# A list scheduler's price for a change of ScalarE's table, raised in two places

## The chip, the cores and the metric

One core of a Trainium2 chip runs the whole program. The metric is the device time of one execution in microseconds (us), as the median of several runs. The core has five engines that run their own instruction streams side by side: TensorE (PE in the profile, with its weight loads as PEld), VectorE (DVE), ScalarE (ACT), GpSimd (POOL) and SyncE (SP, which here issues DMAs).

## The reference

Four attention modules follow each other on x, which holds 32 sequences of 64 tokens with 256 features, all in float32. A second input, ctx, has the same shape. In short:

```
x = L0(x, ctx)        # norm, 8 heads of 64, softmax, output product, residual
x = L1(x, ctx)        # 16 heads of 16; keys and values from layer_norm(ctx); gated residual
x = L2(ctx, x)        # queries from x, keys and values from concat(ctx, x); then
                      #   rmsnorm and gelu(out @ w1 + b1) @ w2 + b2, residual
x = L3(x, ctx)        # layer norm and masked self-attention; layer norm and
                      #   cross-attention; layer norm and gelu perceptron, residuals
softmax: exp(scores - max) / sum
gelu:    the tanh form; w1 is 256 x 1024, w2 is 1024 x 256
```

So Exp is wanted by every softmax, and GELU by the two perceptrons, those of L2 and of L3. L2's rmsnorm takes a Square.

## The kernel before

**Stages.** L0 is written in an order laid out by hand, with the set-up of later weights mixed in. Everything after it, the modules L1, L2 and L3 (L3's self-attention and its cross-attention count apart, so that there are four layers l = 0 to 3 of the loop), is first recorded and then ordered by a planner, the class `Plan`. In the trace that part begins at about 455 us.

**Groups and sets.** The 2048 tokens are cut into 8 groups of 256. Attention is done in 80 "sets" of 128 tokens: 16 for L1, 32 for L2, 16 for L3's self-attention, 16 for its cross-attention. A set runs through scores on TensorE (`a_scores`, four PSUM banks "s"), for L3 a mask (`a_mask`, VectorE and GpSimd), the maximum (`a_max`), the subtraction (`a_sub`), one Exp of 128x1024 on ScalarE (`a_exp`), the sum (`a_sum`), scaling (`a_scale`, GpSimd, or `a_rows`), transposes (`a_turn`), the product with the values (`a_values`) and the way out (`a_fin`). Three tiles "E" serve the sets in turn.

**Perceptrons.** `mlp_steps` makes four steps for each group of L2 and of L3, so 64 in all. A step's `up` makes a product into a PSUM bank of the "pj" ring, of which there are four, applies GELU to it in two ACTIVATEs of 128x256 (tile "u"), casts it on ScalarE (xThh) and takes the rest on VectorE (xTlh). Its `down` makes the second product, which adds up over the four steps. L2's rmsnorm ahead of its perceptron (`post_b`) has two Squares in a group (tile "rb" from "boot").

**The planner.** `link` turns the recorded operations into atoms with their dependencies, `cost` gives each atom a duration, and, on ScalarE, a form: "gelu" for GELU, "exp" for Exp and Square, none for copies and for the plain ACTIVATEs. `order` then builds the program: it keeps a clock of its own for each engine (`free`), and for every engine it looks at the atoms whose dependencies are placed. A candidate's start is the latest of the engine's clock, its inputs and the freeing of its tiles. On ScalarE a candidate whose form differs from the one last placed gets an addition to its start. The earliest start wins on each engine; among equal starts the due date decides (`urgent`, with a random part of up to 0.5 from a fixed seed, 4), and over the engines the earliest again. When the atom is placed and the form changes, a second addition goes to its start, which moves ScalarE's clock and all that depends on the atom. So both additions count in the planner's clock, and the first counts in the comparison too. The planner's times never reach the chip: they only fix each engine's order of instructions, which the chip then follows with its own durations. The loads of the tables themselves aren't written by the kernel; they are put in where the order needs them.

The same order binds TensorE, VectorE, ScalarE, GpSimd and the DMA issues of SyncE. Weights of later layers are loaded and prepared in the course of it (`load_unit`: DMA, scaling on GpSimd, a cast on ScalarE, the rest on GpSimd or VectorE), at sets fixed by `load_at`.

Of the kernel before, what the change touches and what calls it, by code (L numbers as in the profile page):

```python
# [93 lines left out]
class Plan:  # L94
# [194 lines left out]
    def order(self, atoms):  # L289
        ties = random.Random(self.SEED)  # L290
        first, left, queue, turn = {}, {}, {}, {}
        for at in atoms:
            at.takes, at.written = [], False
            for r in at.roots:
                r.__dict__.setdefault("users", []).append(at)
                if r not in first and r.at is None:
                    first[r] = at
                left[r] = left.get(r, 0) + 1

        for r, at in first.items():  # L300
            src = [b for b in at.before if b.root is not None and b.root.psum and b.key == "T" and not r.psum] if at.key != "T" else []
            owner = src[-1] if src else at
            r.owner = owner
            owner.takes.append(r)
        for at in atoms:
            for r in at.takes:
                queue.setdefault(r.slot, []).append(r)
        for at in atoms:
            at.takes += [r for r in at.roots if r.at is None and r not in at.takes]
        live = {slot: list(rs) for slot, rs in self.early.items()}  # L310
        gone = {r: 0.0 for rs in live.values() for r in rs if r not in left}
        free = {k: 0.0 for k in self.engines}
        form = {}
        ready = {k: [] for k in self.engines}
        for at in atoms:
            at.wait = len(at.before)
            at.at = 0.0
            at.urgent = at.due + ties.uniform(0, self.TIE) - (3.0 if at.key in "VA" and any(isinstance(x, View) and x.root.psum for o in at.ops for x in o.ins) else 0.0)
            if not at.wait:
                ready[at.key].append(at)  # L320
        out = []

        def slots(at):

            t = 0.0
            need = {}
            at.takes = [r for r in at.takes if r.at is None]
            if at.key == "T" and any(r.tag == "pj" for r in at.takes) and len(at.root.users) > 1:
                us = at.root.users
                if not us[1].key == "T" and any(not x.written and x not in us for b in us for x in b.before):  # L330
                    return None
            for r in at.takes:
                need.setdefault(r.slot, []).append(r)
            for s, rs in need.items():
                q = queue[s]
                if any(r not in q[:self.RING.get(s[1], 1) + len(rs) - 1] for r in rs):
                    return None
                have = live.setdefault(s, [])
                over = len(have) + len(rs) - rs[0].bufs
                if over > 0:  # L340
                    ends = sorted(gone[r] for r in have if r in gone)
                    if len(ends) < over:
                        return None
                    t = max(t, ends[over - 1])
            return t
        n = len(atoms)
        while len(out) < n:
            best = None
            for e, rs in ready.items():
                cand = []  # L350
                for at in rs:
                    s = slots(at)
                    if s is None:
                        continue
                    t = max(free[e], at.at, s)
                    if at.form is not None and e == "A" and form.get(e) not in (None, at.form):
                        t += 0.4
                    cand.append((t, at))
                if not cand:
                    continue  # L360
                t0 = min(t for t, _ in cand)
                t, at = min(((t, at) for t, at in cand if t <= t0), key=lambda x: (x[1].urgent, x[1].index))
                if best is None or t < best[0]:
                    best = (t, at)
            if best is None:
                stuck = [(k, at.due, at.ops[0].method, [r.slot for r in at.takes]) for k, rs in ready.items() for at in rs]
                raise RuntimeError(f"no order: {len(out)} of {n}, {stuck[:20]}")
            t, at = best
            e = at.key
            ready[e].remove(at)  # L370
            d = at.time
            if at.form is not None:
                if form.get(e) not in (None, at.form):
                    d += 0.12 if e == "T" else 0.0
                    if e == "A":
                        t += 0.9
                form[e] = at.form
            for r in at.takes:
                have = live[r.slot]
                if len(have) >= r.bufs:  # L380
                    old = min((x for x in have if x in gone), key=lambda x: gone[x])
                    have.remove(old)
                    r.at = old.at
                else:
                    r.at = min(set(range(r.bufs)) - {x.at for x in have})
                have.append(r)
                queue[r.slot].remove(r)
            at.start = t
            free[e] = t + d
            end = t + d + at.late  # L390
            at.end = end
            for r in at.roots:
                left[r] -= 1
                r.last = max(getattr(r, "last", 0.0), end)
                if not left[r]:
                    gone[r] = r.last
            for b in at.after:
                b.wait -= 1
                b.at = max(b.at, (t + d if b.key == e else end) + 0.06 * (b.key != e))
                if not b.wait:  # L400
                    ready[b.key].append(b)
            at.written = True
            out.append(at)
        self.atoms = out
        return out
# [1269 lines left out]
```

## Time and profile before

| what | value |
|---|---|
| median of 3 runs | 1130.74 us (1130.67 to 1131.31) |
| the profiled execution | 1132.07 us |
| its span | 1130.3 us, 35569 instructions |
| mean granted clock of TensorE | 0.987 |
| busy: PE, DVE, ACT, POOL | 1067.8, 894.9, 906.3, 761.8 us |
| loads of ScalarE's table in the planned part | 45, together 57.7 us |
| DMA | 41.21 MB, mean 36 GB/s |

The page gives each engine's busy time, the span in 40 slices (28.3 us each), the chain of work that ended last and the costliest groups. In a group's line the name of the operation is followed by what it writes and reads, the count, the busy time in us, the mean in ns, and the idle time of the engine just before these instructions. L156 marks the instructions of L0 and L125 those that went through the planner's recorder. A busy TensorE isn't a TensorE at its peak, since the ends of its matmuls are modelled.

### The profile page before, as it was taken

Reading aid. Unit: us, or ns where it says so; the run is one execution under the profiler, and the core shown is the slowest. Engines: PE = TensorE matmul, PEld = TensorE weight load, DVE = VectorE, ACT = ScalarE, POOL = GpSimd, SP = SyncE. Lnnn points to the kernel's source line nnn. Section 1 sums busy time; section 2 is a strip of 40 time slices with the busy share of each in tenths; the row PEclk is TensorE's granted clock in tenths of the full one; section 3 lists DMA queues with packets and bytes.
Section 4 is the critical chain, followed back from the end, with each engine's and each line's share of the span. In section 5 each row is a group of like instructions: output and inputs, shape, how many; then the busy total and the mean of one; then the engine's idle time right before and its main releaser. Section 6 shows DMA issues by size and latency. Waiting matters only on the chain.

```text
span 1130.3 us, 35569 instructions
## 1 busy us (share of the span) xinstructions
PE 1067.8 (94%) x14396; PEld 872.2 (77%) x14396; DVE 894.9 (79%) x1575; ACT 906.3 (80%) x2326; POOL 761.8 (67%) x829
## 2 busy tenths in 40 slices
PE   6999999999999999899999999999999988889998
PEld 4666666666666666788898989998988877779998
DVE  4889989897888777688888878777878878777842
ACT  2888888887888789577778889889898777888974
POOL 3788888886778667635546634477866989996520
PEclk9999999999999999899999999999999989989999
DMA  3001211111110100311211100000000111110000
GB/s 96 21 25 36 61 35 49 35 34 44 34 34 25 34 16 2 93 37 58 68 47 47 34 26 26 21 29 22 21 20 21 49 51 51 43 34 21 11 20 29
DMA packets 41300, 41.21 MB, mean 36 GB/s; under 512 B 7059, under 2 KB 37796, under 8 KB 41136
## 3 DMA queue, kind: packets, MB, share of 16 engines
q1 hardware_dynamic: 40816, 38.54, 10.9%
q8 instruction: 114, 1.87, 0.7%
q10 hardware_dynamic: 320, 0.40, 0.1%
q14 instruction: 50, 0.41, 0.1%
HBM read 26.30 MB, written 2.10 MB: 25 GB/s over the span
## 4 chain that ended last, share of the span: by engine, by line
PE 59%; DVE 15%; ACT 10%; POOL 10%; issue 4%; DMA 0%; SPq 0%; DVEq 0%; POOLq 0%; ACTq 0%
PE pj L125 39%; PE pt L156 6%; ACT E L156 5%; PE av L156 5%; PE sc L156 4%; PE s L125 4%; DVE mx L156 3%; POOL E L125 3%; DVE E L125 2%; DVE PT L156 2%; ACT PT L156 2%; DVE sB L156 2%; POOL E L156 2%; DVE mx L125 2%; PE pt L125 1%
## 5 line engine op out<-in xcount | busy, mean ns | idle before, releaser
L156 POOL TENSOR_TENSOR E<-E,rs 128x512 f32<-128x512 f32 x256 | 263.5, 1040 | 84.0 <-DVE rs L156 64.5
L156 ACT ACTIVATE E<-sc,mx 128x256 f32<-128x256 f32 x512 | 238.4, 481 | 23.2 <-DVE rs L156 21.9
L156 DVE TENSOR_REDUCE mx<-sc 128x4 f32<-128x1024 f32 x128 | 155.8, 1217 | 2.8 <-PE sc L156 1.4
L156 PE MATMUL sc<-cd,T 64*128 64x256 f32 x1024 | 144.0, 400 | 10.5 <-ACT E L156 10.0
L125 POOL TENSOR_TENSOR E<-E,sm 128x512 f32<-128x512 f32 x96 | 101.1, 1078 | 68.9 <-DVE sm L125 56.1
L156 PE MATMUL av<-PT,us 128*64 128x256 f32 x1024 | 125.0, 385 | 0.0
L156 PEld LDWEIGHTS pt<-ident,E 64*128 64x128 f32 x2048 | 83.6, 139 | 43.6 <-POOL E L156 15.8
L156 PEld LDWEIGHTS av<-PT,us 128*64 128x64 f32 x1024 | 68.3, 136 | 54.7 <-issue 20.4
L156 PEld LDWEIGHTS sc<-cd,T 64*128 64x128 f32 x1024 | 89.6, 189 | 25.8 <-ACT E L156 17.8
L125 DVE TENSOR_REDUCE sm<-E 128x16 f32<-128x1024 f32 (+1 forms) x80 | 96.0, 1200 | 15.3 <-ACT E L125 15.3
L156 ACT ACTIVATION_READ_ACCUMULATOR E<-sc,mx 128x1 f32 x512 | 108.0, 211 | 0.0
L156 PE MATMUL pt<-ident,E 64*128 64x64 f32 x2048 | 98.2, 228 | 6.1 <-ACT PT L156 2.2
L125 ACT COPY PTe<-pj 128x512 f32<-128x512 f32 x160 | 88.0, 590 | 19.2 <-PE pj L125 17.1
L125 PE MATMUL pj<-ident,E 128*128 128x128 f32 x640 | 90.8, 281 | 8.0 <-DVE rb L125 2.5
L156 ACT COPY PT<-pt 128x512 f32<-128x512 f32 x128 | 75.6, 591 | 24.3 <-PE pt L156 22.8
L125 PE MATMUL pj<-w,xThh 128*128 128x256 f32 x512 | 93.4, 287 | 0.1
L125 PE MATMUL pj<-xThn,w 128*128 128x256 f32 x512 | 92.2, 285 | 0.7 <-DVE rb L125 0.4
L156 DVE COPY PT<-pt 128x512 f32<-128x512 f32 x128 | 86.0, 672 | 5.2 <-PE pt L156 5.1
L125 ACT ACTIVATE E<-E 128x1024 f32<-128x1024 f32 x80 | 84.9, 1062 | 5.8 <-DVE E L125 4.6
L125 PEld LDWEIGHTS pj<-ident,E 128*128 128x128 f32 x640 | 71.6, 143 | 16.7 <-issue 3.6
L125 DVE TENSOR_TENSOR xTlh<-u,xThh 128x512 fp32r<-128x512 f32 x64 | 54.8, 861 | 29.9 <-ACT xThh L125 29.5
L156 DVE RECIPROCAL rs<-sm 128x2 f32<-128x2 f32 x256 | 40.1, 156 | 46.5 <-ACT E L156 43.7
(223 smaller groups left out, 2798.3 us busy)
## 6 DMA issues: line engine op xcount, KB each, us to landing
kb<-kfm SPq DMA_DIRECT2D x44, 128.0 KB
xd<-in_x SPq DMA_DIRECT2D x32, 128.0 KB
cd<-in_ctx SPq DMA_DIRECT2D x32, 128.0 KB
boot<-in_ctxT SPq DMA_DIRECT2D x16, 256.0 KB
kb<-kfm SPq DMA_DIRECT2D x64, 64.0 KB
xt<-in_x SPq DMA_DIRECT2D x16, 128.0 KB
boot<-in_ctx SPq DMA_DIRECT2D x8, 256.0 KB
out<-x SPq DMA_DIRECT2D x8, 256.0 KB
```

Of the source, the lines that this page charges most:

```text
L125: getattr(self.engines[o.key], o.method)(*[real(x) for x in o.p], **{k: real(x) for k, x in o.k.items()})
L156: return f(*p, **k)
```

## The change

Two numbers in `order`. The addition in the comparison goes from 0.4 to 0.9 us, the addition when the atom is placed from 0.9 to 1.28 us. In all a change of the table moves the planner's clock by 2.18 us where it moved it by 1.3. Nothing else in the source differs; the order of all instructions after L0 is worked out anew from these numbers, with the same seed.

```diff
                     t = max(free[e], at.at, s)
                     if at.form is not None and e == "A" and form.get(e) not in (None, at.form):
-                        t += 0.4
+                        t += 0.9
                     cand.append((t, at))
...
                 if form.get(e) not in (None, at.form):
                     d += 0.12 if e == "T" else 0.0
                     if e == "A":
-                        t += 0.9
+                        t += 1.28
                 form[e] = at.form
```

## The prediction

> **What bounds the kernel now.** I read the page first: busy times and the 40 slices.
>
> ```profile
> PE 1067.8 (94%) x14396; PEld 872.2 (77%) x14396; DVE 894.9 (79%) x1575; ACT 906.3 (80%) x2326; POOL 761.8 (67%) x829
> ...
> PE   6999999999999999899999999999999988889998
> ...
> POOL 3788888886778667635546634477866989996520
> PEclk9999999999999999899999999999999989989999
> ```
>
> TensorE (PE) is busy in all but the last tenth of nearly every slice; the exceptions lie around slice 16 (where layer 0 ends, 455 us) and in slices 32 to 35, where POOL rises to 9 and the granted clock falls. Only what stands after 455 us is ordered by the planner, so I cut that part by what ScalarE (ACT) does in it, in the view of busy time by stretch:
>
> ```profile
> 455.00:600.00 145.00, 137.18 (x2544) 121.97 (x2546) 119.42 (x172) 102.63 (x210) 78.11 (x89) 0.98 0.19 59
> 600.00:875.00 275.00, 268.99 (x4293) 245.38 (x4281) 219.90 (x319) 242.85 (x471) 166.18 (x167) 1.00 0.08 26
> 875.00:1010.00 135.00, 118.97 (x1723) 104.90 (x1722) 105.46 (x169) 105.34 (x220) 126.48 (x128) 0.92 0.14 45
> 1010.00:1061.00 51.00, 50.04 (x656) 47.33 (x655) 43.25 (x55) 46.08 (x85) 36.62 (x31) 1.00 0.06 19
> 1061.00:1130.30 69.30, 65.28 (x630) 64.14 (x630) 29.91 (x52) 42.60 (x88) 13.43 (x20) 0.99 0.07 24
> ```
>
> After the stretch and its length the columns are busy PE, weight loads, DVE, ACT, POOL, the clock, the DMA share and GB/s. The reader should see three kinds of stage. From 600 to 875 attention and the layer-2 perceptron run mixed: PE idles 6.0 us of 275 (2.2%). From 455 to 600 there is attention with no GELU: PE idles 7.8 of 145 (5.4%). From 875 to 1010 POOL holds the pace (126.5 of 135): PE idles 16.0, and the clock of 0.92 takes another 135 x 0.08 = 10.8 us of full-speed work away.
>
> Next the groups of ScalarE after 455 us, for the operation that the change is about, and its line of time:
>
> ```profile
> L125 ACT ACT_TABLE_LOAD x45 | 57.7, 1283 | 1.2 <-DVE E L125 0.5
> ```
>
> ```profile
> 749.09 0.42 ACT L125 ACTIVATE rb<-boot 128x256 f32<-128x256 f32 x1
> 749.41 0.19 ACT L125 ACTIVATION_READ_ACCUMULATOR rb<-boot 128x1 f32 x1
> 749.62 1.28 ACT L125 ACT_TABLE_LOAD   x1
> 750.91 1.06 ACT L125 ACTIVATE E<-E 128x1024 f32<-128x1024 f32 x1
> 752.00 0.59 ACT L125 CAST xTh<-pj 128x512 fp32r<-128x512 f32 x1
> 752.60 1.28 ACT L125 ACT_TABLE_LOAD   x1
> 753.90 0.84 ACT L125 ACTIVATE u<-pj,vecs 128x256 f32<-128x256 f32 x2
> ```
>
> A switch takes 1.28 us and the next ACTIVATE starts 0.01 to 0.02 us behind it. Here two switches enclose a single Exp. Also, the Square (rb) ran with the GELU table loaded and called for no load; the load came only for the Exp.
>
> Last, the chain that ended last, for which of the 45 loads lie on the path. Four pieces do: 1.28 us at 616.85, 0.49 at 827.68, and these two:
>
> ```profile
> 853.46 1.28 ACT L125
> ...
> 860.33 1.28 ACT L125
> ```
>
> That is 4.33 of 57.7 us, 7.5%. The other 53.4 us lie beside PE's work.
>
> **The change part by part.** No operation is added or dropped except table loads; matmuls, evictions and DMAs stay, and all of them after 455 us may change places, on the queues of SP and POOL too.
>
> *The model's charge.* A switch cost the planner 0.4 (added to the start with which it competes, and kept) + 0.9 = 1.3 us, within 0.02 of the trace's 1.283. It will cost 0.9 + 1.28 = 2.18. So the sum becomes wrong by 0.9 us a switch, 40 us over 45, while the comparison (0.4, now 0.9) comes nearer to the truth. This costs nothing on the chip by itself; it moves other engines' work in the written order.
>
> *Fewer loads.* A GELU, while Exp's table is in, is taken only if ScalarE has nothing else to start within 0.9 us instead of 0.4, and likewise back. In ScalarE's timeline from 600 to 866 us I counted 25 idle gaps of 0.4 us or more, but only 6 of 0.9; from 866 to 1010 us 24 and 11. A quarter to a half of the chances remain, but work held back makes gaps of its own, so the count of loads lies between 45 and about 11 (a quarter). I take a fifth away, 9 loads, nearer to the present number because the 64 GELU steps (two ACTIVATEs each) must all pass sooner or later. That frees 9 x 1.283 = 11.5 us of ScalarE; at the chain's 7.5% it is -0.9 us of span. Bounds: 0 and -4.3 (all four pieces).
>
> *A rule against the trace.* The Trainium skill (ScalarE: Activation LUTs, "What ACT_TABLE_LOAD costs") puts a switch at about 2.66 us, 1.28 for the load and 1.38 for a drain, and its rule is to batch by table. The rows above show the load's 1.28 and no drain. By the page 9 loads would free 24 us, and on the same 7.5% give -1.8 us.
>
> *Work that is held.* Whoever waits longer for the switch is the GELU, behind it the cast xThh, DVE's xTlh and the second product of the perceptron; its PSUM bank, one of four "pj" banks, stays taken meanwhile. In the other direction Exp waits, and sum, scaling, transposes and values behind it. Square is counted as Exp's table by the planner, so it too is held, for a load that the trace shows it doesn't need; it opens each of the eight perceptrons of layer 2. What hides a held step now is PE's other ready work. If the perceptron is not there to fill, the stage drifts from 2.2% idle toward the 5.4% of the stage without GELU: 275 x (0.054 - 0.022) = +8.8 us at most, 0 at least. I take half, +4.4 us, as the higher barrier holds some of the fill and not all.
>
> *The POOL-held stage.* One perceptron step is 24 matmuls, which in the tail took 1071.61 to 1074.34, 2.73 us. A layer-2 step that is late enough to fall into 875 to 973, where no GELU runs now and PE idles, saves 2.73; a layer-3 step that leaves 973 to 1010 for the tail costs 2.73. Eight GELU ACTIVATEs, four steps, run there now: at most 4 x 2.73 = +10.9 us. In the other direction three steps are -8.2 us. I enter 0, since the stage's own pace is POOL's and the change removes no POOL work. The clock belongs to this: the stretch 988 to 996 had 0.57, 8 x 0.43 = 3.4 us lost; one such stretch more or less is +-3.4, entered as 0.
>
> *Sum.* -0.9 + 4.4 = +3.5 us. The profiled execution took 1132.07 (span 1130.30, 1.77 around it), so it would be 1135.6; it lies 1.33 above the median of the runs, and on the median the forecast is 1130.74 + 3.5 = 1134.2.
>
> **The rivals.**
>
> *Faster: the late perceptron becomes the filler of the POOL-held stage.* For it: ScalarE is 88% busy from 600 to 875 and long gaps are rare there, so that is where GELUs are held; attention, which needs POOL and DVE, moves ahead while POOL has room (166 of 275), and pure PE work lands where PE idles. The last layer-2 GELU runs at 862 us, when 24 of the 80 Exps are still to come, so there is slack to be late. Against: each group's perceptron must end before its norm in the next layer, and the urgent dates that break ties are unchanged. Price: two steps -5.5, loads -0.9, half the holding cost +2.2: -4.2, 1126.5 us; three steps, loads and no holding cost give -9.1, 1121.6. It decides once the steps moved outweigh the holding cost, that is from two steps on.
>
> *Much slower: layer 3's first perceptrons leave the POOL-held stage.* +10.9 and the forecast's +3.5: 1145.1 us. Against it: ScalarE has 11 gaps of 0.9 us there, so the switch at 973.30 should still be found.
>
> *No effect on time:* loads go, as the change says, but all of them from under PE, and the places that idle trade equal amounts: 1130.7 us.
>
> **How the numbers follow.** The forecast has 0.42, the faster rival 0.38, the much slower one 0.08, no effect 0.12. A measurement of this kernel can tell about 0.2%, 2.3 us. Of the forecast's case 0.04 falls inside that, of the faster one's 0.02, of the last one 0.08 (0.02 beyond on each side). Faster 0.36 + 0.02 = 0.38; same 0.14; slower 0.38 + 0.08 + 0.02 = 0.48. The range goes from the faster rival's far end to just past the much slower one, 1121 to 1146; the forecast alone holds 1131 to 1140.
>
> **What would show it.** Fewer than 45 table loads, about 36; stretches between loads longer. PE's idle time from 600 us to the end of layer 2's GELUs above 2.2% confirms the holding cost; below 2% refutes it. If the last "u<-pj,vecs" comes later than 862.7 and PE idles clearly under 16 us in the POOL-held stage, the faster rival is right. If layer 3's first "u<-pj,b" moves from 974.6 past 1010 behind a longer all-PE tail, the much slower one is. The forecast is wrong altogether if the loads stay at 45, or if PE's busy time itself changes by several us, for nothing above prices that.

## The result, and the profile after

The changed kernel takes 1144.49 us (median of 4 runs, 1143.94 to 1144.71) against 1131.03 for the kernel before on the same chip: a ratio of 1.0118, 95% interval 1.0106 to 1.0131, 13.5 us slower. Its profiled execution took 1144.59 us with a span of 1142.9, 12.6 us longer than the span before.

The page of the changed kernel, busy times, two rows of the slices and the shares of the chain:

```profile
PE 1065.7 (93%) x14396; PEld 867.2 (76%) x14396; DVE 894.4 (78%) x1575; ACT 888.2 (78%) x2312; POOL 761.9 (67%) x829
...
PE   6899999999999999899999999999999978899998
...
PEclk9899999999999999999999999999999999999999
...
PE 53%; DVE 19%; ACT 11%; POOL 11%; issue 5%; DMA 1%; SPq 0%; DVEq 0%; POOLq 0%; ACTq 0%
```

ScalarE is 18 us less busy, with 14 instructions fewer, and TensorE's busy time hardly moves (1067.8 before). The chain has changed hands in part: 53% of a longer span lie on PE (59% before), 19% on DVE (15% before). The same stages, cut at the same times (busy PE, weight loads, DVE, ACT, POOL, clock, DMA share, GB/s):

```profile
455.00:600.00 145.00, 137.19 (x2563) 121.15 (x2562) 120.81 (x174) 103.70 (x212) 80.94 (x92) 1.00 0.19 62
600.00:875.00 275.00, 260.78 (x4078) 237.04 (x4078) 210.14 (x305) 221.39 (x441) 155.72 (x164) 1.00 0.08 25
875.00:1010.00 135.00, 118.63 (x1828) 103.89 (x1826) 112.74 (x178) 108.29 (x230) 129.29 (x123) 0.96 0.15 47
1010.00:1061.00 51.00, 47.26 (x678) 42.82 (x677) 39.85 (x52) 41.37 (x82) 42.50 (x38) 1.00 0.06 19
1061.00:1142.90 81.90, 76.56 (x724) 75.03 (x722) 35.40 (x59) 48.05 (x98) 15.57 (x21) 0.99 0.06 21
```

PE's idle time, stretch less busy, was 7.8, 6.0, 16.0, 1.0 and 4.0 us before, 34.8 in all. It is now 7.8, 14.2, 16.4, 3.7 and 5.3, 47.5 in all (sums taken before rounding). The 12.6 us more are the whole of the longer span. Most of it, 8.2 us, arises from 600 to 875, the stage in which GELU and Exp are mixed. The stretches are equal in time, not in work: when the last GELU of L2 starts (862.73 us before, 865.53 now), 56 of the 80 Exps were done before and 53 are now.

ScalarE's groups after 455 us, the loads:

```profile
L125 ACT ACT_TABLE_LOAD x31 | 39.8, 1283 | 0.5
```

31 loads instead of 45: 17.9 us of ScalarE's time are gone, with each load still 1283 ns. ScalarE doesn't use them. From 600 to 870 us its timeline has 48 idle gaps of 0.4 us or more and 19 of 0.9, where 25 and 6 had been.

One place shows what goes wrong. ScalarE's line of time has three Exps back to back behind a load:

```profile
699.47 1.28 ACT L125 ACT_TABLE_LOAD   x1
700.76 2.95 ACT L125 ACTIVATE E<-E 128x1024 f32<-128x1024 f32 x3
```

Two of these sets had their subtraction (E<-s,mx) long behind them, and VectorE had stood idle for 3.16 us, waiting for scores, just before the load ran:

```profile
682.91 1.23 DVE L125 TENSOR_TENSOR E<-s,mx 128x1024 f32<-128x1024 f32 x1
...
690.06 1.22 DVE L125 TENSOR_TENSOR E<-s,mx 128x1024 f32<-128x1024 f32 x1
...
699.34 1.23 DVE L125 TENSOR_REDUCE mx<-s 128x8 f32<-128x1024 f32 x1 [3.16 <-PE s L125]
```

The chain of the changed kernel runs through VectorE just there, and TensorE has two gaps:

```profile
699.34 1.24 DVE mx L125
...
700.67 1.23 DVE E L125
701.89 0.60 DVE x L125
702.49 1.14 DVE sm L125
...
703.65 0.20 DVE sm L125
703.86 1.33 DVE boot L125 x2
705.19 1.13 DVE sm L125
706.32 0.61 DVE xTla L125
```

```profile
705.25 0.66 PE L125 MATMUL pj<-ident,boot 128*128 128x128 f32 x4 [1.07 <-DVE boot L125]
...
706.97 0.50 PE L125 MATMUL pj<-xTha,w 128*128 128x256 f32 x2 [0.17 <-DVE xTla L125]
```

Two sets had waited 16.6 and 10.4 us for their Exps, most of it with GELU's table in; the third set's subtraction ended at 701.89, in time to follow them without a pause. On VectorE their sums ("sm") then meet the maximum and subtraction of the third set, a residual, a norm ("boot") and a split ("xTla"): 7.6 us in a row, and TensorE waits for the norm (1.07 us) and the split (0.17 us). From 686 to 720 us the chain of the kernel before had only PE in it. Over 600 to 875 us the products into the "pj" banks held 79.6% of the chain before and 60.3% now.

### The profile page after: what moved, and what is told of

It is laid out like the page before. It is cut to its first block, busy times and chain, and to the rows that moved or that the text cites. A ratio compares the mean times of both kernels' runs of the same rounds, so it can differ in the third digit from the quotient of the medians.

```text
span 1142.9 us, 35554 instructions
## 1 busy us (share of the span) xinstructions
PE 1065.7 (93%) x14396; PEld 867.2 (76%) x14396; DVE 894.4 (78%) x1575; ACT 888.2 (78%) x2312; POOL 761.9 (67%) x829
## 3 DMA queue, kind: packets, MB, share of 16 engines
q1 hardware_dynamic: 40816, 38.54, 10.7%
## 4 chain that ended last, share of the span: by engine, by line
PE 53%; DVE 19%; ACT 11%; POOL 11%; issue 5%; DMA 1%; SPq 0%; DVEq 0%; POOLq 0%; ACTq 0%
PE pj L125 33%; PE pt L156 7%; ACT E L156 5%; POOL E L125 5%; PE av L156 5%; PE sc L156 4%; PE s L125 4%; DVE mx L156 3%; DVE E L125 3%; DVE PT L156 2%; DVE mx L125 2%; ACT PT L156 2%; DVE sB L156 2%; POOL E L156 2%; DVE sm L125 1%
## 5 line engine op out<-in xcount | busy, mean ns | idle before, releaser
L125 PE MATMUL pj<-ident,E 128*128 128x128 f32 x640 | 93.1, 282 | 15.7 <-ACT E L125 3.3
L125 DVE TENSOR_TENSOR xTlh<-u,xThh 128x512 fp32r<-128x512 f32 x64 | 52.9, 830 | 41.7 <-ACT xThh L125 41.6
L125 PEld LDWEIGHTS pj<-xThn,w 128*128 128x128 f32 x512 | 72.3, 188 | 7.9 <-ACT PTe L125 1.9
```

The source lines that it names most:

```text
L125: getattr(self.engines[o.key], o.method)(*[real(x) for x in o.p], **{k: real(x) for k, x in o.k.items()})
```

## The experiments

All are the kernel before with the two numbers of `order`, or what stands beside them, altered. The first four take the change apart. "The comparison" is the first number, "the charge" what a switch costs the planner in all.

**The comparison alone** (`cmp_alone`).

```diff
-                        t += 0.4
+                        t += 0.9
...
-                        t += 0.9
+                        t += 0.38
```

> Only the comparison is raised: 0.9 where it compares and 0.38 when the atom is placed, so that the planner's charge for a switch stays at 1.28 us (1.3 before). Theory hold (the higher barrier holds GELU and Exp back, and TensorE lacks filler): loads fall as in the changed kernel, to 31 to 35, and the time rises by 8 us or more, 1139 or above. Theory charge (a planner's clock that is wrong by 0.9 us a switch misplaces the other engines' work): loads may fall, the time stays within 3 us of before, 1131 to 1134. Theory re-deal (any new order loses about as much against an old one that happened to be good): 1134 to 1145, with no relation to the loads.

1150.33 us, ratio 1.0177 (1.0153 to 1.0202). Its loads and two stages:

```profile
L125 ACT ACT_TABLE_LOAD x37 | 47.5, 1283 | 0.6
...
600.00:875.00 275.00, 266.96 (x4202) 243.61 (x4200) 217.60 (x309) 229.50 (x456) 161.49 (x164) 0.99 0.08 26
...
1010.00:1061.00 51.00, 43.41 (x609) 38.50 (x608) 39.22 (x52) 41.98 (x77) 36.82 (x36) 0.98 0.06 19
```

The theory of the charge alone falls: a charge that is right to 0.02 us loses more than the change. The theory of held work has the time, but not the loads (31 to 35 were expected) and not the place: the stage that it points to idles only 8.0 us, and 7.6 us of idle time stand in the short stage from 1010 to 1061 (1.0 before).

**The charge alone** (`charge_alone`).

```diff
-                        t += 0.9
+                        t += 1.78
```

> Only the charge is raised: 0.4 where it compares, 1.78 when the atom is placed, 2.18 us in all as in the changed kernel. Hold: loads stay near 45 (42 to 47), TensorE idles about as before from 600 to 875 us (6 us), the time is 1129 to 1134. Charge: 8 us or more are lost, 1139 or above, with loads near 45. Re-deal: 1134 to 1145, whatever the loads.

1149.78 us, 1.0168 (1.0146 to 1.0189).

```profile
L125 ACT ACT_TABLE_LOAD x37 | 47.5, 1283 | 0.6
...
600.00:875.00 275.00, 257.72 (x4010) 234.33 (x4007) 209.94 (x300) 227.91 (x445) 156.91 (x160) 0.99 0.08 24
```

My expectation of "hold", loads near 45, was wrong, and so were the loads near 45 of "charge", which had the time: with the comparison untouched the loads fell to 37, and PE idles 17.3 us from 600 to 875. So the charge works as a barrier too. That it does so by making ScalarE look late, so that more candidates stand ready when it comes free, is my reading of the code and wasn't tried.

**The new numbers in one half only** (`l2_only`, then `l3_only`). The planner counts the GELUs that it has placed; 64 belong to L2.

```diff
+        gelus = 0
...
-                        t += 0.4
+                        t += 0.9 if gelus < 64 else 0.4
...
-                        t += 0.9
+                        t += 1.28 if gelus < 64 else 0.9
                 form[e] = at.form
+                gelus += at.form == "gelu"
```

> The two new numbers hold only until the 64 GELUs of L2's perceptron are placed; from there the planner has the old ones. Up to about 868 us the order is that of the changed kernel. Hold: TensorE idles some 14 us from 600 to 875 as in the changed kernel (6.0 before), and what follows is as before, so 8 of the 13.5 us remain, 1139 (1136 to 1142). Re-deal: what follows is another draw, anywhere from 1134 to 1148.

1145.35 us, 1.0131 (1.0114 to 1.0149): more than the 1139 that "hold" expected, and inside the 1134 to 1148 of "re-deal". PE idles 14.5 us from 600 to 875, as in the changed kernel, so that stage is reproduced; but with the old numbers behind it the rest idles 27.2 us, no less than with the new ones (25.4; 21.0 before). Its work arrives three sets late, as in the changed kernel (53 Exps at L2's last GELU).

> The other half: the old numbers until the 64 GELUs of L2 are placed, the new ones for the rest. The order up to about 865 us is that of before. Hold: the stages behind 875 us lose the 4.4 us that TensorE's idle time grew there in the changed kernel, 1135 (1133 to 1138), and the first GELU of L3 comes later than 974.6 us. Re-deal: anywhere from 1128 to 1140. If L2's part alone were to blame: 1131.

1136.19 us, 1.0049 (1.0033 to 1.0065), by a condition turned round (`gelus >= 64`).

```profile
L125 ACT ACT_TABLE_LOAD x41 | 52.6, 1283 | 1.2 <-DVE E L125 0.5
...
600.00:875.00 275.00, 269.02 (x4289) 245.18 (x4287) 220.11 (x318) 241.71 (x468) 166.61 (x167) 1.00 0.08 26
875.00:1010.00 135.00, 120.04 (x1754) 106.77 (x1742) 109.50 (x175) 106.70 (x227) 128.91 (x128) 0.95 0.15 46
1010.00:1061.00 51.00, 46.68 (x658) 41.97 (x657) 37.52 (x53) 40.56 (x74) 33.93 (x32) 0.97 0.06 18
1061.00:1133.80 72.80, 67.42 (x618) 65.88 (x618) 29.90 (x49) 43.41 (x89) 13.03 (x19) 0.99 0.07 23
```

As "hold" expected: the first stage is that of before to 0.03 us, and the last three idle 15.0 + 4.3 + 5.4 = 24.7 us against 21.0. L3's first GELU moves from 974.6 to 989.4 us. The time alone would fit "re-deal" (1128 to 1140) too. L2's part is the larger one, and the two do not add up: 14.8 and 5.7 us apart, 13.5 together.

**Is it the numbers or the draw?** A new order is also a new draw. Only the seed was changed, `SEED, TIE = 1, 0.5` and `5, 0.5`, with the old numbers (`before_s1`, `before_s5`) and with the new ones (`after_s1`, `after_s5`).

> The old numbers (0.4 and 0.9) with the seed of the due dates' random part at 1 instead of 4. Numbers theory (the new numbers make a worse order, whatever the seed): within 5 us of before, 1126 to 1136, with 42 to 48 loads. Draw theory (the old order with seed 4 was a good draw, and any new draw loses about as much as the change did): 1137 to 1150, although the planner's numbers are the old ones.

1138.67 us, 1.0080 (1.0055 to 1.0105), 49 loads.

> The old numbers with seed 5. Numbers theory: 1126 to 1136 with 42 to 48 loads. Draw theory: 1137 to 1150.

1132.81 us, 1.0015 (1.0005 to 1.0025), 43 loads.

> The new numbers (0.9 and 1.28) with seed 1. Numbers theory: 8 to 15 us above the run of the old numbers with seed 1, about 31 loads. Draw theory: no steady sign against the old numbers with seed 1, 1137 to 1150, and about 31 loads.

1173.79 us, 1.0370 (1.0336 to 1.0404), 35 loads.

> The new numbers with seed 5. Numbers theory: 8 to 15 us above the run of the old numbers with seed 5. Draw theory: between 8 us below and 8 us above it, 1137 to 1150.

1159.60 us, 1.0259 (1.0239 to 1.0279), 31 loads.

Seed by seed the new numbers cost 13.5, 35.1 and 26.8 us (seeds 4, 1, 5). The draw theory falls as the whole cause: it had no steady sign, and the old numbers stay within 8 us of each other and below every order with the new ones. It did have before_s1, which lies in its band. "Numbers" has the sign, but not the sizes: before_s1 lies 2.7 us and one load above its band, and two of the differences are twice the 8 to 15 that it gave. So a draw is worth up to 8 us with the old numbers and 29 with the new, and of the three seeds 4 is the kindest to the change. What the two slow orders look like, after_s1 in the last two stages:

```profile
1010.00:1061.00 51.00, 39.78 (x507) 35.52 (x506) 36.86 (x43) 36.68 (x74) 44.42 (x43) 0.93 0.08 25
1061.00:1167.50 106.50, 95.79 (x975) 91.25 (x973) 48.33 (x78) 62.39 (x124) 23.75 (x28) 0.99 0.06 19
```

11.2 and 10.7 us of idle time, where the kernel before has 1.0 and 4.0.

**The other way** (`lower`). 0.2 in the comparison and 0.45 at the placing, so that a switch is charged at half of what it takes.

> Both numbers go the other way from the old ones: 0.2 where it compares and 0.45 when the atom is placed, seed 4; the planner then charges 0.65 us for a switch that takes 1.28. Numbers theory in its plain form (the more a switch is charged, the more GELUs and Exps are held): loads rise to 50 or more, TensorE idles 6 us or less from 600 to 875, and the time is at or below before, 1126 to 1133. Truth theory (the planner's order is best where its charge agrees with the chip, and worsens to both sides): loads of 50 or more that the planner did not reckon with, 1136 to 1145.

1139.27 us, 1.0064 (1.0046 to 1.0082), 47 loads, 6.3 us of idle time from 600 to 875. Neither theory wins. The loads stay short of the 50 that both expected; the time is what "truth" gave, but it is also no more than 0.6 us above the old numbers' worst seed, and the stage of the mixed tables idles as little as before. Cheaper is not better, and no harm of the size of the change either.

**One direction only** (`to_gelu_only`, then `to_exp_only`).

```diff
-                        t += 0.4
+                        t += 0.9 if at.form == "gelu" else 0.4
...
-                        t += 0.9
+                        t += 1.28 if at.form == "gelu" else 0.9
```

> The new numbers only for the switch to GELU's table; the way back to Exp's keeps the old ones. If it is the held perceptron that leaves TensorE without filler: most of the loss, 1140 or above. If it is the held Exp, with the attention behind it, that costs: within 4 us of before, 1127 to 1135. If only the sum of the two charges counts: about half, 1136 to 1140. Loads between 35 and 42 in each case.

1148.81 us, 1.0149 (1.0130 to 1.0167), 37 loads.

> The mirror image: the new numbers only for the way back to Exp's table. Held perceptron: within 4 us of before, 1127 to 1135. Held Exp: 1140 or above. Only the sum: 1136 to 1140. Loads between 35 and 42.

1146.18 us, 1.0116 (1.0100 to 1.0133), 35 loads; 0.4 and 0.9 for GELU, 0.9 and 1.28 for Exp.

None of the three theories fits both runs: "held perceptron" had the second at 1135 at most, "held Exp" the first, and "only the sum" both at 1140 at most. Whichever of the two tables is held back, the loss is as large as with both. My reading, which these runs don't prove, is that a barrier on one way delays the round trip, and with it both kinds of work.

**Square without a form** (`square_free`). Old numbers, seed 4; in `cost` Square no longer counts as Exp's table.

```diff
-            exp = any(x == AF.Exp or x == AF.Square for x in o.p)
+            exp = any(x == AF.Exp for x in o.p)
```

(Its duration in the model was kept.)

> The old numbers (0.4 and 0.9, seed 4), but the planner no longer counts Square with Exp's table: Square gets no form, as copies have none, since the traces show it run with either table loaded. If holding Square back, which opens each of L2's perceptrons, is a part of what charging a switch costs: at or below before, 1124 to 1131, and the stage of L2's perceptrons ends earlier than 862.7 us. If it is one more order with the old charge: 1131 to 1140, as the old numbers gave with three seeds. Loads between 41 and 49 either way.

1139.74 us, 1.0079 (1.0062 to 1.0096), 43 loads, and L2's last GELU at 862.69: one more order of the old charge. So nothing is seen of a gain from Square's needless wait in the model; one order can't show it if it is smaller than the scatter of 8 us. No version here beats the kernel before.

All orders side by side, by loads; idle is PE's from 455 us to the end of the profiled span, us the median:

| kernel | comparison, placing | loads | PE idle | us |
|---|---|---|---|---|
| before_s1 | 0.4, 0.9 | 49 | 41.4 | 1138.7 |
| lower | 0.2, 0.45 | 47 | 39.3 | 1139.3 |
| before | 0.4, 0.9 | 45 | 34.8 | 1131.0 |
| before_s5 | 0.4, 0.9 | 43 | 38.3 | 1132.8 |
| square_free | 0.4, 0.9 | 43 | 41.6 | 1139.7 |
| l3_only | new in L3 | 41 | 38.4 | 1136.2 |
| cmp_alone | 0.9, 0.38 | 37 | 46.2 | 1150.3 |
| charge_alone | 0.4, 1.78 | 37 | 49.3 | 1149.8 |
| to_gelu_only | new to GELU | 37 | 49.1 | 1148.8 |
| to_exp_only | new to Exp | 35 | 48.7 | 1146.2 |
| l2_only | new in L2 | 35 | 49.6 | 1145.4 |
| after_s1 | 0.9, 1.28 | 35 | 63.4 | 1173.8 |
| after | 0.9, 1.28 | 31 | 47.5 | 1144.5 |
| after_s5 | 0.9, 1.28 | 31 | 54.6 | 1159.6 |

Every order with 37 loads or fewer takes 1144 us or more and idles 46 us or more; every one with 41 or more takes 1140 or less and idles 42 or less. The six of the second kind are six different orders (one of them, l3_only, with the new numbers behind L2), so a new order as such doesn't cost what the higher price costs.

The traces show the held work too. Between a set's subtraction and its Exp lie, in the mean over the Exps from the first to the last GELU of L2, 4.6 to 6.0 us in the six orders with 41 loads or more and 6.9 to 8.3 us in the eight with 37 or fewer (5.6 before, 7.0 in the changed kernel; the subtractions and the Exps are paired in their order).

Idle time isn't all of the loss in the slowest orders. The span of after_s1 is 30.6 us longer than that of before_s1: 22.0 us are idle time of PE, and the other 8.6 are longer busy time (649.1 against 640.5 us from 455 us on). For seed 5 it is 16.3 and 10.6 of 26.9. Why PE is busy for longer there stays open.

The Trainium skill (ScalarE: Activation LUTs, "Table sets: the hidden batching unit") advises batching activations by table. In these runs fewer loads went with a longer time: ScalarE isn't the bound here (12% idle from 600 to 875 us before, PE 2.2%), and the orders in which work waited longer for its table are those in which TensorE idles more.

## Why the prediction was right, and where its sizes were off

- *Direction and mechanism:* right. Fewer loads free ScalarE, which isn't the bound, and holding work back leaves TensorE without any. But the rise of 13.5 us is nearly four times the 3.5 forecast, and 1144.5 lies outside the 1131 to 1140 that the forecast alone held. That the range has it, near its upper end, is owed to the much slower rival, which was given 0.08 and whose account holds only in part: so far that is luck.
- *Fewer loads, -0.9 us:* 9 loads were guessed to go, 14 did. That the freed time lies beside PE's work was right in kind: ScalarE's gaps grew instead. Even the -0.9 isn't seen: the chain of the changed kernel goes through four whole loads (664.30, 759.10, 1005.15 and 1057.72 us), 5.12 us against 4.33.
- *Held work, +4.4 us of at most 8.8:* the mis-sized term. The stage measured +8.2, nearly the upper bound. Taking half had no row behind it. The bound itself, the idle share of the stage without GELU, was a good one for this order, though not for all: charge_alone adds 11.3. By the sign that the prediction named, idle time from 600 us to the end of L2's GELUs, all of the drift took place, from 2.2% to 5.4%:

```profile
600.00:862.73 262.73, 256.90 (x4112) 234.10 (x4100) 209.14 (x302) 232.52 (x451) 158.82 (x163) 1.00 0.08 26
...
600.00:865.53 265.53, 251.31 (x3947) 228.35 (x3947) 203.41 (x292) 212.28 (x424) 153.17 (x160) 1.00 0.08 25
```

- *The POOL-held stage, entered as 0:* the second mis-sized term. Its own idle time stayed (16.0 to 16.4), but the stages behind it lost 2.8 and 1.3 us. Of the much slower rival, the move took place in part: L3's first GELU came at 1006.45 us instead of 974.59, not past the 1010 that the sign asked for, and five of the eight GELU ACTIVATEs still started in the stage. After the last Exp there were 42 GELU ACTIVATEs against 32, five steps more, where four had been priced at 10.9 us. That price did not appear as idle time in the stage: it held 18 Exps instead of 15, three sets late from L2, and these, as I read it, filled it. That the rival's sum of 1145.1 lies so near is chance: by the accounts above most of the loss arises earlier.
- *The faster rival:* L2's last GELU came 2.8 us later and none fell into the POOL-held stage beyond 875 us.
- *The planner's sum being wrong, at no cost:* wrong. charge_alone shows that a charge at the placing alone costs as much as the comparison alone, 19.2 against 19.8 us. The step treated it as a shift of names; it is a second barrier.
- *Square held for nothing:* true in the code, without effect that these runs can tell.
- *The drain of 1.38 us that the Trainium skill (ScalarE: Activation LUTs, "What ACT_TABLE_LOAD costs") adds to a load:* not in the changed kernel either. The load of 699.47 starts 0.02 us behind the ACTIVATE ahead of it, ends at 700.75, and the Exp starts at 700.76.

What stays open is the last link: why the same barrier costs 13.5 us with one seed and 35.1 with another. That the price makes the loss is shown; that the way from held work to idle TensorE is bunching on VectorE is shown at one place, and that it makes up all of the 12.6 us isn't. More buffers for the sets in flight, which would tell bunching from other causes, weren't tried.

## What to carry to other kernels

In this list scheduler a price for a mode change also rations it, wherever it is put; here, where the engine that changes mode doesn't set the end, all eight orders with a price raised while L2 was placed were slower than all six others. Count the bounding engine's idle time before counting the loads saved. And try an edit of a heuristic with several seeds: here one seed shows 13.5 us, three show 13.5 to 35, against a scatter of 8 with nothing else changed.

## What the runs showed of the hardware that was not expected

In the stage held by POOL (875 to 1010 us) the mean granted clock was 0.92 before and 0.96 in the changed kernel, over 135 us 5.4 us more of full speed. PE's busy time there moved by 0.34 us only (118.97 to 118.63), with 6% more matmuls in it (1828 against 1723).

The mean clock over the whole span, 0.987 before and 0.992 in the changed kernel, can't be put down to the change. The kernel before, whose order is the same in every execution, had 0.984 (1134.52 us), 0.987 (1130.57 us) and 0.992 (1129.75 us) in three executions on one chip. The changed kernel, which idles 12.6 us more, had 0.990 to 0.992 in its four executions.
